# Weighing values in 64 by 32 tiles, and exchanging softmax statistics by ScalarE copies

## The chip, the cores and the metric

The kernel runs on one core of a Trainium2 chip. A core has a matrix engine (TensorE, "PE" in the profile, with its weight loads as "PEld"), VectorE (DVE), ScalarE (ACT) and GpSimd (POOL), each with its own queue of instructions that it works through in order, and SyncE (SP), which issues most DMAs here. The engines wait for each other by semaphores. The metric is the time of one execution in microseconds. Before the change it is 1120.16 us, the median of three runs (1119.69 to 1120.71).

## The reference

A transformer block over x of shape (2, 1024, 256), all in fp32, with 16 heads of 64 and a context of 154 rows of 192:

```python
h = _layernorm(x, ln1_g, ln1_b)
x = _attention(h, h, sa_wq, sa_wk, sa_wv, sa_wo, sa_bo) + x
h = _layernorm(x, ln2_g, ln2_b)
x = _attention(h, cond_emb, ca_wq, ca_wk, ca_wv, ca_wo, ca_bo) + x
h = _layernorm(x, ln3_g, ln3_b)
p = h @ ff_w1 + ff_b1
a, gate = (p[..., :D_FF], p[..., D_FF:])
h = a * jax.nn.gelu(gate, approximate=False) @ ff_w2 + ff_b2
return h + x
```

Attention is the usual one: scores q k^T / 8, softmax over the keys, and the weights times the values, for each head; then the output projection and its bias. The change lies in the self-attention, where queries and keys are both the 1024 rows.

## The kernel before

Heads are worked on in pairs: 2 batches times 8 pairs are 16 units. A unit is two halves of 512 queries, and a half is four slots (`SH`), so the self-attention has 16 x 8 = 128 slots (`SA`). One slot takes 128 queries, in two groups of 64 (`scores`, called twice). A group's score tile has 128 partitions, four quarters of 32. Quarter a4 holds 32 queries against one half of the keys: quarters 0 and 1 hold the same 32 queries against keys 0 to 511 and 512 to 1023, and quarters 2 and 3 do the same for the next 32 queries. So each query's softmax is spread over two neighbouring quarters, and their maxima and sums have to be brought together. The score matmuls use TensorE as 8 tiles of 64 rows by 32 columns (L483).

A slot goes through these steps:

- TensorE: scores of both groups into two PSUM tiles (`ps_s`, two buffers, so scores of the next slot wait for this slot's exponentials).
- VectorE: negated maxima of both groups into `st` (L645, in `self_first`).
- ScalarE: four exponentials with these maxima as bias; each also sums its output (L494, `exponents`, with a record of its own for reading the accumulator). Maxima and sums stand in `st[:, 0]`, eight numbers per partition.
- `exchange`: each quarter gets its neighbour's eight numbers in `st[:, 1]`, by four DMAs on SyncE's queue (L504).
- `join`, one slot later: GpSimd forms the differences of the maxima (`dd`, L512 to L514), ScalarE their exponentials (`ee`, L516), GpSimd the joint sums (`zz` L518, `den` L520).
- `reciprocals`, after that slot's transposes: VectorE's `rd` (L591), then GpSimd scales the four blocks of exponentials in place (L595).
- `turn_groups`, another slot later: VectorE transposes them in 32 by 32 blocks into `pT` (L609).
- `weigh`: when a half is done, its values are weighed in two parts (`self_values`, L530), in slots 2 and 3 of the next half. The operands' partitions pair query quarters with keys, so `v` is held twice, once with its partition halves swapped. Before the change the tiles are 64 by 64: for each key block four matmuls, two row halves by two heads.

Nothing reorders the work: the loop over p writes the order of each engine's queue by hand (`manual_schedule`). In slot p TensorE does the scores of p and then either weighing, or a piece of other work (projections of queries, keys and values of the next unit, L352 and L383; output projections, L457; layer-norm transposes, L270). VectorE's order is: maxima of p, transposes of p-2's exponentials, an addition of an output projection to `x` where there is one (L464), `rd` of p-1, layer-norm statistics where there are some (L230, L231, L246). ScalarE's order is: copies of the last piece of work out of PSUM (`stores`, such as L367, L375, L392, L630), exponentials of p, `ee` of p-1. `then` in `self_first` writes the order of `exponents`, `scale_groups` (which calls `join`) and `exchange`.

SyncE's queue also carries the loads of weights ahead of their use, and the swaps of `v`'s halves (L399, L400).

After the self-attention come the cross-attention (48 slots) and the feed-forward; neither is changed.

Of the kernel before, what the change touches and what calls it, by code (L numbers as in the profile page):

```python
# [18 lines left out]
def tile_transformer_block(ctx: ExitStack, tc: tile.TileContext, a: dict, out: bass.AP):  # L19
    nc = tc.nc  # L20
# [7 lines left out]
    DH = 64  # L28
# [11 lines left out]
    KB = 32  # L40
# [3 lines left out]
    QG = 2 * KB  # L44
    TP = NB * KB
    NM = P // QG
    QH = S // 2
    GH = QH // QG
    NK = HB // KB
# [45 lines left out]
    row_of, r = {}, 0  # L95
# [10 lines left out]
    for n in names[:2]:  # L106
        for r0 in range(0, P, HR):
            (nc.scalar if n == names[0] else nc.sync).dma_start(
                out=cols[r0:r0 + HR, row_of[n]:row_of[n] + NH],
                in_=w[n].rearrange("(r p) -> p r", p=HR),  # L110
# [365 lines left out]
    def scores(u, q, k, g):  # L476
        sc = ps_s.tile([P, 2, HB], F32, tag="s", name=f"s_{u}")
        for a4 in range(4):
            a2, h = divmod(a4, 2)
            for j in range(2):  # L480
                r = slice(j * DH, (j + 1) * DH)
                c = g * QG + a2 * KB
                nc.tensor.matmul(  # L483
                    sc[a4 * KB:(a4 + 1) * KB, j, :], lhsT=q[r, c:c + KB],
                    rhs=k[r, h * HB:(h + 1) * HB], start=True, stop=True,
                    tile_position=(j * DH, a4 * KB),
                )
        return sc

    def exponents(u, sc, st, i):  # L490

        pr = pp_.tile([P, 2, HB], F32, tag="P", name=f"p_{u}")
        for j in range(2):
            nc.scalar.activation(  # L494
                pr[:, j, :], sc[:, j, :], AF.Exp, bias=st[:, 0, 0, i, j:j + 1],
                accum_out=st[:, 0, 1, i, j:j + 1],
            )
        return pr

    def exchange(st):  # L500

        for a4 in range(4):
            o4 = a4 ^ 1
            nc.sync.dma_start(  # L504
                out=st[a4 * KB:(a4 + 1) * KB, 1], in_=st[o4 * KB:(o4 + 1) * KB, 0]
            )

    def join(u, st):

        dd = small.tile([P, 2, 4], F32, tag="dd", name=f"dd_{u}")  # L510
        neg = st[:, :, 0].rearrange("p s i j -> p s (i j)")
        nc.gpsimd.tensor_tensor(dd[:, 0, :], neg[:, 1, :], neg[:, 0, :], ALU.subtract)  # L512
        nc.gpsimd.tensor_tensor(dd[:, 1, :], neg[:, 0, :], neg[:, 1, :], ALU.subtract)
        nc.gpsimd.tensor_scalar(dd, dd, 0.0, 1.0, op0=ALU.min, op1=ALU.mult)  # L514
        ee = small.tile([P, 2, 4], F32, tag="ee", name=f"ee_{u}")
        nc.scalar.activation(ee, dd, AF.Exp)  # L516
        zz = small.tile([P, 2, 4], F32, tag="zz", name=f"zz_{u}")
        nc.gpsimd.tensor_tensor(zz, ee, st[:, :, 1].rearrange("p s i j -> p s (i j)"), ALU.mult)  # L518
        den = small.tile([P, 4], F32, tag="den", name=f"den_{u}")
        nc.gpsimd.tensor_tensor(den, zz[:, 0, :], zz[:, 1, :], ALU.add)  # L520
        return ee, den

    def weigh(po, v, pT, t):

        for e in range(2):
            for a2 in range(2):
                r = slice(a2 * QG, (a2 + 1) * QG)
                n = 2 * t + (e ^ a2)
                for j in range(2):
                    nc.tensor.matmul(  # L530
                        po[a2][j * DH:(j + 1) * DH, :QH // 2],
                        lhsT=v[r, t, e, j * DH:(j + 1) * DH], rhs=pT[r, j * NK + n, :],
                        start=(t == 0 and e == 0), stop=(t == NT - 1 and e == 1),
                        tile_position=(a2 * QG, j * DH),
                    )


# [47 lines left out]
    def scale_groups(u, st, members):  # L585

        ee, den = join(u, st)

        def reciprocals():
            rd = small.tile([P, 4], F32, tag="rd", name=f"rd_{u}")  # L590
            nc.vector.reciprocal(rd, den)  # L591
            for i, pr in enumerate(members):
                for j in range(2):
                    c = 2 * i + j
                    nc.gpsimd.tensor_scalar(  # L595
                        pr[:, j, :], pr[:, j, :], rd[:, c:c + 1], ee[:, 0, c:c + 1],
                        op0=ALU.mult, op1=ALU.mult,
                    )
                groups.append(pr)

        return reciprocals
# [11 lines left out]
    def self_values(h, part):  # L613

        b, pr = units[h // 2]
        if part == 0:
            bank = sum_tile if h < 2 * NU - 1 else mm_tile
            halves[h, "po"] = [bank(f"po_{h}_{a2}") for a2 in range(2)]
            if pr % HP == 0 and h % 2 == 0:
                oT["sa", b, pr // HP] = pt_.tile([P, HP, S], F32, tag="oT", name=f"o_sa{b}_{pr}")  # L620
        po = halves[h, "po"]
        for t in range(NT // 2 * part, NT // 2 * (part + 1)):
            weigh(po, qk["sa", b, pr][2], halves[h], t)
        if part == 0:
            return None
        dst = oT["sa", b, pr // HP][:, pr % HP, (h % 2) * QH:(h % 2 + 1) * QH]

        def store():
            for a2 in range(2):
                nc.scalar.copy(  # L630
                    dst.rearrange("p (g a i) -> p g a i", a=2, i=KB)[:, :, a2, :],
                    po[a2][:, :QH // 2].rearrange("p (g i) -> p g i", i=KB),
                )

        return store

    def self_first(p):

        b, pr = units[p // (2 * SH)]
        g = p % (2 * SH)  # L640
        q, k, _ = qk["sa", b, pr]
        st = small.tile([P, 2, 2, 2, 2], F32, tag="st8", name=f"st_{p}")
        sc = [scores(f"{p}_{i}", q, k, 2 * g + i) for i in range(2)]
        for i in range(2):
            nc.vector.tensor_reduce(st[:, 0, 0, i, :], sc[i], AX.X, ALU.max, negate=True)  # L645

        def then():
            members = [exponents(f"{p}_{i}", sc[i], st, i) for i in range(2)]
            late = scale_groups(*joins.pop(0)) if joins else None
            exchange(st)  # L650
            joins.append((p, st, members))
            return late

        return then
# [323 lines left out]
    with tc.manual_schedule():  # L978
# [57 lines left out]
        for p in range(SA):  # L1036
# [21 lines left out]
            if h == 0 or hg < LAG:  # L1058
# [4 lines left out]
                ui, n = divmod(p, 2 * SH)  # L1063
# [8 lines left out]
        for c in range(CA):  # L1072
# [13 lines left out]
            ui, n = divmod(c, len(CG))  # L1086
# [52 lines left out]
            elif n == 2:  # L1139
# [3 lines left out]
                elif ui == HP:  # L1143
                    wo["ca"] = const.tile([P, NPAIR, D], F32, tag="wo", name="ca_wo")
                    later[:0] = [lambda i=i: nc.sync.dma_start(
                        out=wo["ca"][:, i, :], in_=w["ca_wo"][i * P:(i + 1) * P, :])
# [65 lines left out]
```

## Time and profile before

| | |
|---|---|
| median of three runs | 1120.16 us |
| the profiled execution, its own time | 1119.22 us |
| its span, first to last instruction | 1117.4 us |
| TensorE busy | 1103.5 us (99%) |
| VectorE busy | 855.7 us (77%) |
| GpSimd busy | 681.0 us (61%) |
| ScalarE busy | 629.5 us (56%) |
| scores L483, 4096 records | 251.6 us |
| weighing L530, 4096 records | 235.8 us |
| exponentials L494, 512 | 344.8 us |
| scalings L595, 512 | 385.6 us |
| transposes L609, 256 | 302.2 us |
| maxima L645, 256 | 301.1 us |
| `st<-st` DMAs, 512 | 1.0 KB each, 1.8 us to landing |
| granted TensorE clock | 1.000 |

Busy time of a group is the union of its instructions' time, and "mean" is that of one instruction. Matmuls overlap in the array: a matmul record of 64x512 has a mean of 594 ns, yet 32 of them start and pass in under 2 us. So for TensorE the distance from one start to the next says more than durations. An fp32 matmul of the program shows as two records, each with a weight load. The first maxima of the self-attention start at 18.8 us, the last at 715.8 us. In the stretch from 20 to 717 us TensorE is busy for 692.5 us, VectorE for 630.5, GpSimd for 520.7 and ScalarE for 460.7. In the timeline, instructions of one kind that follow each other are merged into a line with their count.

### The profile page before, as it was taken

Reading aid. Unit: us, or ns where it says so; the run is one execution under the profiler, and the core shown is the slowest. Engines: PE = TensorE matmul, PEld = TensorE weight load, DVE = VectorE, ACT = ScalarE, POOL = GpSimd, SP = SyncE. Lnnn points to the kernel's source line nnn. Section 1 sums busy time; section 2 is a strip of 40 time slices with the busy share of each in tenths; the row PEclk is TensorE's granted clock in tenths of the full one; section 3 lists DMA queues with packets and bytes.
Section 4 is the critical chain, followed back from the end, with each engine's and each line's share of the span. In section 5 each row is a group of like instructions: output and inputs, shape, how many; then the busy total and the mean of one; then the engine's idle time right before and its main releaser. Section 6 shows DMA issues by size and latency. Waiting matters only on the chain.

```text
span 1117.4 us, 36668 instructions
## 1 busy us (share of the span) xinstructions
PE 1103.5 (99%) x14340; PEld 686.5 (61%) x14340; DVE 855.7 (77%) x1205; ACT 629.5 (56%) x2030; POOL 681.0 (61%) x1584
## 2 busy tenths in 40 slices
PE   8999999999999999999999999999999999999998
PEld 5445545545545455455455455476776777888887
DVE  4889999898998899999989989868777875412212
ACT  4666666766666666667666765665555553121111
POOL 2777777777777777777777777766656653220000
PEclk9999999999999999999999999999999999999999
DMA  3222212111111012011111111146665453000000
GB/s 85 70 57 50 55 27 51 48 34 41 32 31 42 22 41 46 13 42 39 24 41 32 31 32 26 25 95 158 160 157 125 114 115 79 10 11 10 20 10 19
DMA packets 102318, 59.14 MB, mean 53 GB/s; under 512 B 31994, under 2 KB 92930, under 8 KB 102146
## 3 DMA queue, kind: packets, MB, share of 16 engines
q1 hardware_dynamic: 100914, 56.15, 21.3%
q8 instruction: 113, 1.85, 0.7%
q10 hardware_dynamic: 1232, 0.66, 0.2%
q14 instruction: 59, 0.48, 0.1%
HBM read 27.12 MB, written 2.10 MB: 26 GB/s over the span
## 4 chain that ended last, share of the span: by engine, by line
PE 92%; ACT 2%; DVE 2%; DMA 1%; POOL 1%; SPq 1%; issue 1%; DVEq 0%; ACTq 0%; POOLq 0%
PE s L483 20%; PE po L530 20%; PE pa L933 10%; PE py_sa L457 5%; PE pv_sa L383 5%; PE py_ca L457 5%; PE pf L956 5%; PE pk_sa L352 4%; PE pq_sa L352 4%; PE pq_ca L352 4%; PE poc L851 4%; PE sc L772 3%; ACT p L494 2%; PE ph_ln L270 1%; PE pv_ca L733 1%; DVE st L645 1%
## 5 line engine op out<-in xcount | busy, mean ns | idle before, releaser
L494 ACT ACTIVATE p<-s,st 128x512 f32<-128x512 f32 x512 | 344.8, 686 | 199.0 <-DVE st L645 190.6
L595 POOL TENSOR_SCALAR p<-p,rd,ee 128x512 f32<-128x512 f32 x512 | 385.6, 768 | 47.6 <-DVE rd L591 46.3
L645 DVE TENSOR_REDUCE st<-s 128x2 f32<-128x1024 f32 x256 | 301.1, 1217 | 26.9 <-PE s L483 13.5
L609 DVE STREAM_TRANSPOSE pT<-p 128x1024 f32<-128x1024 f32 x256 | 302.2, 1218 | 0.3 <-POOL p L595 0.3
L483 PE MATMUL s<-k_sa,q_sa 64*32 64x512 f32 x4096 | 251.6, 594 | 5.0 <-ACT p L494 4.3
L530 PE MATMUL po<-pT,v_sa 64*64 64x256 f32 x4096 | 235.8, 380 | 0.9 <-DVE pT L609 0.9
L530 PEld LDWEIGHTS po<-pT,v_sa 64*64 64x64 f32 x4096 | 150.6, 133 | 109.3 <-issue 31.2
L483 PEld LDWEIGHTS s<-k_sa,q_sa 64*32 64x32 f32 x4096 | 66.8, 106 | 126.3 <-issue 68.2
L799 POOL TENSOR_SCALAR p<-p,rden 128x154 f32<-128x154 f32 x256 | 96.8, 399 | 76.0 <-DVE rden L796 75.6
L788 ACT ACTIVATE p<-sc,neg 128x154 f32<-128x154 f32 x256 | 96.1, 405 | 83.3 <-DVE rden L796 78.1
L942 DVE SCALAR_TENSOR_TENSOR u<-pa,cols,gate 128x256 f32<-128x256 f32 x64 | 31.0, 484 | 123.1 <-ACT gate L939 123.1
L933 PE MATMUL pa<-hT_ln,wf 128*128 128x256 f32 x512 | 121.1, 380 | 0.2 <-ACT p L788 0.2
L939 ACT ACTIVATE gate<-pa,cols 128x256 f32<-128x256 f32 x64 | 30.3, 474 | 147.8 <-PE pa L933 146.0
L933 PEld LDWEIGHTS pa<-hT_ln,wf 128*128 128x128 f32 x512 | 96.9, 190 | 13.9 <-issue 0.8
L494 ACT ACTIVATION_READ_ACCUMULATOR p<-s,st 128x1 f32 x512 | 103.8, 203 | 0.0
L383 PEld LDWEIGHTS pv_sa<-sa_wv,hT_ln 64*128 64x128 f32 x1024 | 58.8, 188 | 14.5 <-DMA st<-st 5.9
L518 POOL TENSOR_TENSOR zz<-ee,st 128x8 f32<-128x8 f32 x128 | 25.9, 202 | 65.6 <-ACT ee L516 65.6
L956 PE MATMUL pf<-wf,u 128*128 128x256 f32 x256 | 64.7, 379 | 0.0
L383 PE MATMUL pv_sa<-sa_wv,hT_ln 64*128 64x128 f32 x1024 | 62.0, 276 | 0.2 <-ACT v_sa L392 0.2
L457 PE MATMUL py_sa<-sa_wo,o_sa 128*128 128x256 f32 x256 | 59.7, 386 | 0.0
L457 PE MATMUL py_ca<-ca_wo,o_ca 128*128 128x256 f32 x256 | 59.7, 382 | 0.0
L457 PEld LDWEIGHTS py_sa<-sa_wo,o_sa 128*128 128x128 f32 x256 | 47.4, 190 | 17.8 <-issue 6.2
(87 smaller groups left out, 1250.6 us busy)
## 6 DMA issues: line engine op xcount, KB each, us to landing
wf<-pT_ca SPq DMA_DIRECT2D x128, 128.0 KB, 2.4
st<-st SPq DMA_DIRECT2D x512, 1.0 KB, 1.8
v_sa<-v_sa SPq DMA_DIRECT2D x32, 256.0 KB, 3.5
sa_wq<-in_L_xattn_sa_wq_dram SPq DMA_DIRECT2D x32, 128.0 KB, 2.8
sa_wk<-in_L_xattn_sa_wk_dram SPq DMA_DIRECT2D x32, 128.0 KB, 2.9
sa_wv<-in_L_xattn_sa_wv_dram SPq DMA_DIRECT2D x32, 128.0 KB, 2.9
ca_wq<-in_L_xattn_ca_wq_dram SPq DMA_DIRECT2D x32, 128.0 KB, 3.3
wf<-in_L_xattn_ff_w_dram SPq DMA_DIRECT2D x12, 256.0 KB, 4.2
```

Of the source, the lines that this page charges most:

```text
L352: nc.tensor.matmul(pq[r][f:f + m, at:at + n], lhsT=wt[own, c, f:f + m], rhs=h[own, c, t0:t0 + n], start=(c == 0), stop=(c == NH - 1), tile ...
L383: nc.tensor.matmul(pv[r][:, i * P:(i + 1) * P], lhsT=h[own, c, i * P:(i + 1) * P], rhs=wt[own, c, :], start=(c == 0), stop=(c == NH - 1), ...
L457: nc.tensor.matmul(py[:, e * D:(e + 1) * D], lhsT=o[:, i, (t + e) * P:(t + e + 1) * P], rhs=wo[kind][:, g * HP + i, :], start=(i == 0), st ...
L483: nc.tensor.matmul(sc[a4 * KB:(a4 + 1) * KB, j, :], lhsT=q[r, c:c + KB], rhs=k[r, h * HB:(h + 1) * HB], start=True, stop=True, tile_positi ...
L494: nc.scalar.activation(pr[:, j, :], sc[:, j, :], AF.Exp, bias=st[:, 0, 0, i, j:j + 1], accum_out=st[:, 0, 1, i, j:j + 1],)
L530: nc.tensor.matmul(po[a2][j * DH:(j + 1) * DH, :QH // 2], lhsT=v[r, t, e, j * DH:(j + 1) * DH], rhs=pT[r, j * NK + n, :], start=(t == 0 an ...
L595: nc.gpsimd.tensor_scalar(pr[:, j, :], pr[:, j, :], rd[:, c:c + 1], ee[:, 0, c:c + 1], op0=ALU.mult, op1=ALU.mult,)
L609: nc.vector.transpose(halves[h][:, :, c:c + KB], groups.pop(0).rearrange("p j (n k) -> p (j n) k", k=KB))
L645: nc.vector.tensor_reduce(st[:, 0, 0, i, :], sc[i], AX.X, ALU.max, negate=True)
L799: nc.gpsimd.tensor_scalar(pr_[:, j, i, :T], pr_[:, j, i, :T], rden[:, j, i:i + 1], 1.0, op0=ALU.mult, op1=ALU.mult,)
L933: nc.tensor.matmul(pa[:, half, :TF * P], lhsT=w1[:, c, half * DF + f * P:half * DF + (f + 1) * P], rhs=h[:, c, t0 * P:(t0 + TF) * P], star ...
L956: nc.tensor.matmul(sums[blk][i][:, :D], lhsT=sums[blk, "u"][:, f, i * P:(i + 1) * P], rhs=w2[:, f, :], start=(f == 0), stop=(f == NF - 1),)
```

## The change

Three edits. The exchange is done by ScalarE copies of 32 partitions by 8 elements, where it was done by DMAs. It is called between the exponentials and `scale_groups`, where it was called after both. And the weighing uses tiles of 64 rows by 32 columns, as the scores do: each 64 by 64 matmul becomes two of 64 by 32 with the same moving operand. Numbers of later lines fall by two: L512 to L520 become L510 to L518, L530 becomes L528, L591 becomes L589, L609 becomes L607; L645 becomes L643.

```diff
@@ exchange
         for a4 in range(4):
             o4 = a4 ^ 1
-            nc.sync.dma_start(
-                out=st[a4 * KB:(a4 + 1) * KB, 1], in_=st[o4 * KB:(o4 + 1) * KB, 0]
-            )
+            nc.scalar.copy(st[a4 * KB:(a4 + 1) * KB, 1], st[o4 * KB:(o4 + 1) * KB, 0])
@@ weigh
                 n = 2 * t + (e ^ a2)
-                for j in range(2):
+                for d in range(0, 2 * DH, KB):
                     nc.tensor.matmul(
-                        po[a2][j * DH:(j + 1) * DH, :QH // 2],
-                        lhsT=v[r, t, e, j * DH:(j + 1) * DH], rhs=pT[r, j * NK + n, :],
+                        po[a2][d:d + KB, :QH // 2],
+                        lhsT=v[r, t, e, d:d + KB], rhs=pT[r, d // DH * NK + n, :],
                         start=(t == 0 and e == 0), stop=(t == NT - 1 and e == 1),
-                        tile_position=(a2 * QG, j * DH),
+                        tile_position=(a2 * QG, d),
                     )
@@ self_first, then
             members = [exponents(f"{p}_{i}", sc[i], st, i) for i in range(2)]
+            exchange(st)
             late = scale_groups(*joins.pop(0)) if joins else None
-            exchange(st)
             joins.append((p, st, members))
             return late
```

## The prediction

> **What bounds the kernel now.** I read the chain that ended last first, then the timeline of the self-attention stretch, engine by engine. The page's chain gives its shares by engine and by line:
>
> ```profile
> PE 92%; ACT 2%; DVE 2%; DMA 1%; POOL 1%; SPq 1%; issue 1%; DVEq 0%; ACTq 0%; POOLq 0%
> ```
>
> TensorE is the bound, with 8% left for anything else. The timeline (start in us, length in us, engine, line, instruction, count, and in brackets the idle time before) shows what TensorE does in two slots of one half:
>
> ```profile
> 319.10 1.95 PE L483 MATMUL s<-k_sa,q_sa 64*32 64x512 f32 x32
> 320.97 3.69 PE L530 MATMUL po<-pT,v_sa 64*64 64x256 f32 x64
> 324.59 1.95 PE L483 MATMUL s<-k_sa,q_sa 64*32 64x512 f32 x32
> 326.33 3.64 PE L352 MATMUL pq_sa<-hT_ln,sa_wq 64*32 64x512 f32 x64
> 329.76 1.92 PE L483 MATMUL s<-k_sa,q_sa 64*32 64x512 f32 x32
> 331.48 1.07 PE L352 MATMUL pk_sa<-hT_ln,sa_wk 64*32 64x512 f32 x16
> ```
>
> From start to start: scores ahead of weighing take 1.87 us, weighing 3.62, scores between two projections of their own tile shape 1.72 (329.76 to 331.48), and a projection of 64 records 3.43. Each fp32 matmul leaves two records. The array work of the projection (64 x 512 columns over 8 tiles) equals that of the weighing (64 x 256 over 4).
>
> What is not in the chain, but close behind it, is a loop through the other engines. Here is one slot in which nothing else holds it up:
>
> ```profile
> 287.29 2.36 DVE L645 TENSOR_REDUCE st<-s 128x2 f32<-128x1024 f32 x2
> ...
> 288.55 0.69 ACT L494 ACTIVATE p<-s,st 128x512 f32<-128x512 f32 x1 [1.18 <-DVE st L645]
> ...
> 289.57 2.36 DVE L609 STREAM_TRANSPOSE pT<-p 128x1024 f32<-128x1024 f32 x2
> ...
> 291.12 0.21 ACT L494 ACTIVATION_READ_ACCUMULATOR p<-s,st 128x1 f32 x1
> 291.22 0.22 ACT L516 ACTIVATE ee<-dd 128x8 f32<-128x8 f32 x1
> 291.32 1.08 ACT L375 COPY k_sa<-pk_sa 128x512 f32<-128x512 f32 x2
> ...
> 291.52 0.20 POOL L518 TENSOR_TENSOR zz<-ee,st 128x8 f32<-128x8 f32 x1 [0.57 <-ACT ee L516]
> 291.80 0.20 POOL L520 TENSOR_TENSOR den<-zz 128x4 f32<-128x4 f32 x1
> 292.03 0.18 DVE L591 RECIPROCAL rd<-den 128x4 f32<-128x4 f32 x1
> ...
> 292.33 2.36 DVE L645 TENSOR_REDUCE st<-s 128x2 f32<-128x1024 f32 x2
> ```
>
> The maxima of a slot (L645) release its exponentials; behind them on ScalarE stands `ee` of the slot before; `ee` releases `zz`, `den` and then the reciprocal `rd`; and `rd` stands in VectorE's queue ahead of the next slot's maxima. So the loop closes once per slot and takes 292.33 - 287.29 = 5.04 us. From the first maxima of slot 1 (22.8 us on the timeline) to those of slot 126 (709.7) there are 125 slots in 686.9 us, 5.50 each: the loop has 0.46 us to spare against TensorE.
>
> **The change, part by part.**
>
> *Weighing in 64 by 32 tiles.* Scores and weighing now have one tile shape, so the pair costs 1.72 + 3.43 in place of 1.87 + 3.62: 0.34 us less. Of 64 parts, 62 stand between scores (two are in the cross-attention, beside other shapes): 62 x 0.34 = 21 us, if TensorE remained the bound. The columns streamed stay the same; instructions double to 128 records a part, 27 ns each at 3.43 us. The bounds: at worst a record keeps today's spacing in this line, 3.62 / 64 = 57 ns, and a part takes 7.2 us; at best the part takes 3.43 us. I take the best, because in the scores, whose tile shape this is, the timeline merges 16 weight loads of 106 ns mean into 0.18 us, so starts are about 5 ns apart.
>
> *Exchange: 512 DMAs leave SyncE's queue.* A slot's four took 2.4 to 2.5 us of issue there. Nothing behind them becomes critical by going earlier. One wait goes:
>
> ```profile
> POOL dd L512 <- DMA st<-st: 45.8, 43, 13.7
> ```
>
> It delayed `ee` by about 1 us in a third of the slots. Those delays took the loop over 5.50 us in single slots; TensorE's lead covered nearly all of it, as its 92% says. I count its removal as nothing beyond what the new loop below contains.
>
> *Exchange: four ScalarE copies of 32 partitions by 8 elements per slot.* Their place decides. In the new order they stand on ScalarE between the last exponential and `ee`, inside the loop above. Queued behind them are `ee` and the stores of projections; waiting for `ee` are `zz`, `den`, `rd`, and, behind `rd` on VectorE, the next maxima. Step by step:
> - The first copy reads sums that the last accumulator read writes, and waits for its end: 291.12 + 0.21. A wait for one's own engine costs about 0.08 us (GpSimd: `zz` ends at 291.72, `den` starts at 291.80). So it starts at 291.41, where `ee` started at 291.22, overlapped: 0.19 us.
> - Each copy. The trace has no copy of 8 elements; the nearest in kind are copies to parts of the partitions:
>
> ```profile
> 751.38 0.76 ACT L742 COPY v_ca<-pv_ca 64x256 f32<-64x256 f32 x2
> 752.16 0.36 ACT L743 COPY v_ca<-pv_ca 32x256 f32<-32x256 f32 x1
> ```
>
> These two, then one, start 0.39 us apart, with a mean of 0.368: each begins only after the one before has ended. Copies over all 128 partitions do overlap:
>
> ```profile
> 281.26 0.63 ACT L630 COPY o_sa<-po 128x256 f32<-128x256 f32 x2
> ```
>
> At a mean of 0.372 these start 0.26 apart. A column costs (588 - 372) / 256 = 0.84 ns by the full-width rows, so 8 in place of 256 take 0.21 off: 0.18 us apart without overlap. With overlap it is 0.04 by the same subtraction, or 0.10 by the shortest gap seen in these lines (`ee` to the next copy, 291.22 to 291.32). Between 0.04 and 0.18 I take 0.18, from the rows that are nearest: they too move from one range of partitions to another. `ee`, full width again, follows the fourth after 0.10 to 0.18. Four: 0.69.
> - Sum: 0.19 + 0.69 = 0.88 us. The loop becomes 5.92.
>
> The Trainium skill ("ScalarE: Activation LUTs", section What ACT_TABLE_LOAD costs) gives 186 ns + 0.833 ns per element with immediate operands and says that ACTIVATEs back to back overlap by about 93 ns. By that, an estimate, copies of 8 elements start 0.10 us apart and the loop becomes 5.63; the L742 rows, which do not overlap, speak against applying it here.
>
> *What the loop carries besides.* `rd` used to be ready 0.1 us after the transposes; now VectorE idles about 1 us ahead of it, which hides the `x` additions (L464, 0.65) that stand there. The layer-norm statistics stand behind `rd` and lengthen the loop: 16 tiles in this stretch at 0.399 + 0.182, and 8 offsets at 0.246, about 11 us, some 10 with their overlaps. GpSimd (4 scalings in 3.0, then `dd` in 0.7) is done about 1 us before the late `ee`, so a bias addition of 0.73 still fits.
>
> *Sum.* 125 x 5.92 + 10 = 750 us against 686.9: +63. TensorE's new need, 686.9 - 21 = 666, is 5.33 per slot, below the loop; its saving turns into waiting. The profiled execution took 1119.2 us (span 1117.4), 0.9 under the median of 1120.16. 1119.2 + 63 = 1182; some start-up slots are longer for other reasons, so I say 1181.
>
> **The rivals.**
> - *The copies overlap with a floor of 0.10 us.* Loop 5.04 + 0.19 + 0.40 = 5.63; 125 x 5.63 + 10 = 714: +27, 1146 us. For: full-width copies and `ee` do so. Against: L742 and L743.
> - *The copies stream at 0.04 us, and the kernel ends faster.* Loop 5.04 + 0.19 + 0.16 = 5.39; 674 + 10 = 684: -3 and a bit, 1116 us. It decides from 5.41 us on, that is 0.05 us per copy. For: the slope of the full-width rows. Against: no gap that short in these lines, and the partial copies.
> - *TensorE cannot be fed 128 records a part.* The part decides above 5.92 - 1.72 = 4.2 us, 33 ns per record; at 57 ns a slot takes 1.72 + 7.2 = 8.9, and 62 slots at 3.0 over the loop add 186: about 1367 us. Against: the bursts of loads. For: nothing in this trace sustains 27 ns.
> - The Trainium skill ("TensorE: Matmul & The Clock Gate", section Wait — 56ns, not 53.3ns?) puts the floor between matmul starts at about 25 ns; as an estimate 128 of them are 3.2 us, just inside the 3.43. No row here shows that floor.
>
> **How the numbers follow.** The forecast (copies without overlap) 0.65; overlapping at 0.10 0.20; streaming and faster 0.08; TensorE short of instructions 0.05; the rest 0.02. The range takes in the first two with their bounds: low 1138 (rival one with most statistics hidden), high 1200 (0.15 us more in each slot: copies 0.20 apart, and a second wait of 0.08). A difference under 0.2% is about what a measurement of this kernel can't tell from no change; faster 0.07, same 0.03, slower 0.90.
>
> **What the profile after would show.** Right: maxima about 5.9 us apart in plain slots; `ee` about 0.8 us after the last accumulator read has ended; copies 0.18 us from start to start; VectorE idle about 1 us ahead of `rd`, released by `den`; waits of TensorE's scores for ScalarE; weighing near 3.43 us; no wait of `dd` for a DMA. Wrong: copies 0.1 us apart or less, TensorE still unbroken, or weighing far above 3.43.

## The result, and the profile after

The changed kernel takes 1175.38 us (median of four runs, 1175.11 to 1175.67) against 1119.93 for the kernel before (four runs): 1.0497 times as long, 95% interval 1.0479 to 1.0515. The forecast was 1181 us in a range of 1138 to 1200. The profiled execution took 1175.67 us, its span is 1173.9.

The page's chain that ended last, by engine and by line, has changed hands:

```profile
ACT 38%; PE 35%; DVE 14%; POOL 5%; issue 3%; DMA 0%; SPq 0%; DVEq 0%; ACTq 0%
ACT p L494 27%; DVE st L643 12%; PE pa L931 9%; ACT st L504 7%; PE py_ca L457 5%; PE pf L954 5%; PE pq_ca L352 4%; PE poc L849 3%; PE sc L770 3%; PE pk_sa L352 2%; ACT ee L514 2%; POOL zz L516 2%; POOL den L518 2%; PE s L483 1%; PE pv_ca L731 1%
```

TensorE went from 92% to 35%, which is about the share of the cross-attention and the feed-forward. In the self-attention the chain now runs through the exponentials, the maxima, the copies (L504), `ee`, `zz` and `den`: the loop of the prediction. One slot of it in the timeline:

```profile
316.11 2.36 DVE L643 TENSOR_REDUCE st<-s 128x2 f32<-128x1024 f32 x2
...
317.37 0.69 ACT L494 ACTIVATE p<-s,st 128x512 f32<-128x512 f32 x1 [1.00 <-DVE st L643]
...
318.38 2.36 DVE L607 STREAM_TRANSPOSE pT<-p 128x1024 f32<-128x1024 f32 x2
...
319.94 0.21 ACT L494 ACTIVATION_READ_ACCUMULATOR p<-s,st 128x1 f32 x1
320.19 0.81 ACT L504 COPY st<-st 32x8 f32<-32x8 f32 x4
...
321.03 0.21 ACT L514 ACTIVATE ee<-dd 128x8 f32<-128x8 f32 x1
...
321.32 0.20 POOL L516 TENSOR_TENSOR zz<-ee,st 128x8 f32<-128x8 f32 x1 [1.36 <-ACT ee L514]
321.60 0.20 POOL L518 TENSOR_TENSOR den<-zz 128x4 f32<-128x4 f32 x1
321.83 0.18 DVE L589 RECIPROCAL rd<-den 128x4 f32<-128x4 f32 x1 [1.08 <-POOL den L518]
321.94 2.36 DVE L643 TENSOR_REDUCE st<-s 128x2 f32<-128x1024 f32 x2
```

The period is 321.94 - 316.11 = 5.83 us, where it was 5.04 in an undisturbed slot. Up to the last accumulator read nothing has moved (3.83 us after the maxima, before and after). The copies start 0.04 us after that read has ended and take 0.81; `ee` starts 1.09 after the read's start, where it was 0.10, so it comes 0.99 later. And at the end `rd` to the next maxima takes 0.11 us, where it took 0.30: a gain that the prediction didn't have. From the first maxima of slot 1 (23.19 us) to those of slot 126 (765.05) the stretch takes 741.9 us, against 686.9: 55.0 us more, which is the whole difference between the medians (55.4).

TensorE waits now. From its timeline, and from the list of waits, after and then before (engine, line, for whom, us in total, times, longest):

```profile
321.09 3.67 PE L528 MATMUL po<-pT,v_sa 64*32 64x256 f32 x128
324.70 1.09 PE L483 MATMUL s<-k_sa,q_sa 64*32 64x512 f32 x16
326.04 1.09 PE L483 MATMUL s<-k_sa,q_sa 64*32 64x512 f32 x16 [0.24 <-ACT p L494]
```

```profile
POOL zz L516 <- ACT ee L514: 168.9, 128, 3.9
...
PEld s L483 <- ACT p L494: 151.2, 203, 2.2
...
DVE rd L589 <- POOL den L518: 127.3, 128, 3.6
```

```profile
POOL zz L518 <- ACT ee L516: 65.6, 128, 1.6
...
PEld s L483 <- ACT p L494: 39.2, 87, 2.5
DVE rd L591 <- POOL den L520: 36.2, 55, 3.4
```

The scores of the two groups, one block before, now start 1.34 us apart (324.70 and 326.04): each waits for the exponentials that hold its PSUM buffer. `rd` waits for `den` in every one of the 128 slots, about 1 us each, where it had waited in 55.

### The profile page after: what moved, and what is told of

The parts are those of the page before. It is cut to its first block, busy times and chain, and to the rows that moved or that the text cites. A ratio compares the mean times of both kernels' runs of the same rounds, so it can differ in the third digit from the quotient of the medians.

```text
span 1173.9 us, 43766 instructions
## 1 busy us (share of the span) xinstructions
PE 1129.0 (96%) x18436; PEld 713.3 (61%) x18436; DVE 849.3 (72%) x1205; ACT 734.5 (63%) x2542; POOL 679.2 (58%) x1584
## 4 chain that ended last, share of the span: by engine, by line
ACT 38%; PE 35%; DVE 14%; POOL 5%; issue 3%; DMA 0%; SPq 0%; DVEq 0%; ACTq 0%
ACT p L494 27%; DVE st L643 12%; PE pa L931 9%; ACT st L504 7%; PE py_ca L457 5%; PE pf L954 5%; PE pq_ca L352 4%; PE poc L849 3%; PE sc L770 3%; PE pk_sa L352 2%; ACT ee L514 2%; POOL zz L516 2%; POOL den L518 2%; PE s L483 1%; PE pv_ca L731 1%
## 5 line engine op out<-in xcount | busy, mean ns | idle before, releaser
L483 PE MATMUL s<-k_sa,q_sa 64*32 64x512 f32 x4096 | 283.5, 599 | 26.1 <-ACT p L494 23.7
L643 DVE TENSOR_REDUCE st<-s 128x2 f32<-128x1024 f32 x256 | 300.8, 1216 | 3.4 <-PE s L483 3.0
L607 DVE STREAM_TRANSPOSE pT<-p 128x1024 f32<-128x1024 f32 x256 | 302.3, 1218 | 0.2 <-POOL p L593 0.2
L528 PE MATMUL po<-pT,v_sa 64*32 64x256 f32 x8192 | 242.0, 376 | 0.9 <-DVE pT L607 0.9
L528 PEld LDWEIGHTS po<-pT,v_sa 64*32 64x32 f32 x8192 | 175.4, 106 | 75.2 <-issue 22.7
L483 PEld LDWEIGHTS s<-k_sa,q_sa 64*32 64x32 f32 x4096 | 62.9, 105 | 175.1 <-ACT p L494 151.2
L589 DVE RECIPROCAL rd<-den 128x4 f32<-128x4 f32 x128 | 22.8, 178 | 127.3 <-POOL den L518 127.3
L504 ACT COPY st<-st 32x8 f32<-32x8 f32 x512 | 99.7, 195 | 8.5
L352 PE MATMUL pk_sa<-hT_ln,sa_wk 64*32 64x512 f32 x960 | 61.8, 592 | 6.6 <-ACT q_sa L367 6.6
```

Source lines behind the costliest of these rows:

```text
L352: nc.tensor.matmul(pq[r][f:f + m, at:at + n], lhsT=wt[own, c, f:f + m], rhs=h[own, c, t0:t0 + n], start=(c == 0), stop=(c == NH - 1), tile ...
L483: nc.tensor.matmul(sc[a4 * KB:(a4 + 1) * KB, j, :], lhsT=q[r, c:c + KB], rhs=k[r, h * HB:(h + 1) * HB], start=True, stop=True, tile_positi ...
L504: nc.scalar.copy(st[a4 * KB:(a4 + 1) * KB, 1], st[o4 * KB:(o4 + 1) * KB, 0])
L528: nc.tensor.matmul(po[a2][d:d + KB, :QH // 2], lhsT=v[r, t, e, d:d + KB], rhs=pT[r, d // DH * NK + n, :], start=(t == 0 and e == 0), stop= ...
L607: nc.vector.transpose(halves[h][:, :, c:c + KB], groups.pop(0).rearrange("p j (n k) -> p (j n) k", k=KB))
```

## The experiments

**The tiles alone.** The exchange stays a DMA, in its old place.

```diff
-                for j in range(2):
+                for d in range(0, 2 * DH, KB):
...
-                        tile_position=(a2 * QG, j * DH),
+                        tile_position=(a2 * QG, d),
```

> Only the 64 by 32 tiles of the weighing; the exchange by DMAs and its place stay as before. My theory: the loop through VectorE, ScalarE and GpSimd stays at 5.04 us a slot, below TensorE's new need of 5.33, so most of the 0.34 us for each of 62 parts comes through: 1099 to 1110 us, weighing 3.43 us from start to start. Rival, that 128 records a part cost TensorE more than the shared tile shape saves: 1120 us or above, weighing above 3.6 us.

1115.8 us, ratio 0.9961 (0.9947 to 0.9975): faster, but by 5 us, below what my theory gave. TensorE's part came out as expected, by its timeline:

```profile
322.32 3.66 PE L530 MATMUL po<-pT,v_sa 64*32 64x256 f32 x128
325.77 1.92 PE L483 MATMUL s<-k_sa,q_sa 64*32 64x512 f32 x32
327.49 3.81 PE L352 MATMUL pq_sa<-hT_ln,sa_wq 64*32 64x512 f32 x64
```

Weighing takes 3.45 us from start to start (3.62 before), the scores 1.72. So 128 records pass at 27 ns each, and the rival that they can't is out. What took the rest has no run of its own. The list of waits and the chain name candidates:

```profile
POOL dd L512 <- DMA st<-st: 45.3, 42, 14.2
```

```profile
PE 67%; ACT 8%; DMA 7%; DVE 5%; POOL 5%; SPq 4%; issue 3%; DVEq 0%; POOLq 0%; ACTq 0%
```

The late DMAs of the exchange hold up `dd`, and with it `ee`, in a third of the slots, as they did before. Then TensorE's 5.50 us a slot covered most of that; with less to do it covers less. DMA and its queue now have 11% of the chain in place of 2%, and ScalarE, VectorE and GpSimd together 18% in place of 5%. The prediction had treated those waits as nothing. The loop here also holds the 0.19 us that a later experiment finds. How the loss divides between the two was not measured.

**The copies alone.** Weighing in 64 by 64 tiles.

```diff
-            nc.sync.dma_start(
-                out=st[a4 * KB:(a4 + 1) * KB, 1], in_=st[o4 * KB:(o4 + 1) * KB, 0]
-            )
+            nc.scalar.copy(st[a4 * KB:(a4 + 1) * KB, 1], st[o4 * KB:(o4 + 1) * KB, 0])
...
+            exchange(st)
             late = scale_groups(*joins.pop(0)) if joins else None
-            exchange(st)
```

> Only the exchange by ScalarE copies ahead of the joint exponentials ee; the weighing in 64 by 64 tiles as before. My theory: the loop rules with 5.83 us a slot whatever TensorE saves, so the time is that of the changed kernel: 1172 to 1179 us, copies 0.2 us apart, ee about 0.87 us after the last accumulator read. Rival, that the tiles have a share in the loss: below 1168 us.

1175.44 us, ratio 1.0490 (1.0475 to 1.0506): the changed kernel's time within 0.1 us. The stretch from slot 1 to slot 126 takes 741.8 us against 741.9. The whole loss is the exchange's, and the tiles' gain is fully hidden beneath it.

**The copies behind `ee`.** All of the change, but with the call in its old place.

```diff
             members = [exponents(f"{p}_{i}", sc[i], st, i) for i in range(2)]
-            exchange(st)
             late = scale_groups(*joins.pop(0)) if joins else None
+            exchange(st)
```

> The changed kernel with the copies behind ee in ScalarE's queue, where the DMAs were called before. My theory: it was the place in the loop that cost, not the copies' time; the loop returns to 5.04 less the 0.19 us that the maxima no longer wait for DMA semaphores, 4.85 us, TensorE is the bound again with 5.33 a slot: 1096 to 1106 us. Rival, that 0.8 us more work on ScalarE per slot delays the next exponentials wherever it stands: 1140 us or above.

1107.51 us, ratio 0.9881 (0.9866 to 0.9896). One line's move is worth 68 us: the same copies, as long as before (99.7 us of ScalarE's time in both), cost nothing like that once `ee` doesn't stand behind them. The rival is out. It stays 1.5 us above my range. In the slots with weighing TensorE takes 5.17 us from one part to the next, as it should, but in others it waits for ScalarE's copies out of PSUM, which now stand behind the exchange:

```profile
327.67 3.72 PE L352 MATMUL pk_sa<-hT_ln,sa_wk 64*32 64x512 f32 x57 [0.18 <-ACT q_sa L367]
...
332.85 0.38 PE L528 MATMUL po<-pT,v_sa 64*32 64x256 f32 x1
...
338.02 0.38 PE L528 MATMUL po<-pT,v_sa 64*32 64x256 f32 x1
```

```profile
PEld pk_sa L352 <- ACT q_sa L367: 18.9, 30, 1.4
```

**The same with 64 by 64 tiles.** The edit is the DMA-to-copy one alone, in its old place.

```diff
-            nc.sync.dma_start(
-                out=st[a4 * KB:(a4 + 1) * KB, 1], in_=st[o4 * KB:(o4 + 1) * KB, 0]
-            )
+            nc.scalar.copy(st[a4 * KB:(a4 + 1) * KB, 1], st[o4 * KB:(o4 + 1) * KB, 0])
```

> Copies behind ee as in the run with both, but the weighing in 64 by 64 tiles as before. My theory: TensorE is the bound with 5.50 us a slot, plus the banks that come free later; the late DMAs of before are gone: 1118 to 1130 us, so the tiles are worth 11 to 22 us where the loop is short. Rival, that the gain of the run with both came from the exchange: below 1112 us.

1123.49 us, ratio 1.0022 (1.0013 to 1.0032). So the copies behind `ee` gain nothing by themselves, and the tiles are worth 16.0 us on top of them (1123.49 to 1107.51), 5 us with the DMAs, and nothing with the copies ahead of `ee`. The same edit has three values, by what stands next to it.

**Ahead of the next slot's exponentials.** The copies go where ScalarE waits for the maxima anyway, behind the copies out of PSUM.

```diff
+            if joins:
+                exchange(joins[0][1])
             members = [exponents(f"{p}_{i}", sc[i], st, i) for i in range(2)]
-            exchange(st)
             late = scale_groups(*joins.pop(0)) if joins else None
...
             if c == 0:
+                exchange(joins[0][1])
                 drain.append(scale_groups(*joins.pop(0)))
```

> The changed kernel with a slot's copies ahead of the next slot's exponentials and behind the copies out of PSUM, where ScalarE waits for the maxima anyway. My theory: behind ee the copies delayed the copies out of PSUM, and TensorE waited for their banks about 0.4 us in slots 1 and 4 of each unit; here they delay neither ee nor those: 1096 to 1104 us. Rival, that in slots with long copies out of PSUM they push the exponentials back by as much: 1106 us or above.

1100.43 us, ratio 0.9811 (0.9797 to 0.9826): the fastest of all, 21 us below the kernel before and 75 below the changed one. ScalarE's timeline shows the place:

```profile
321.44 0.21 ACT L514 ACTIVATE ee<-dd 128x8 f32<-128x8 f32 x1
321.54 1.09 ACT L367 ACTIVATE q_sa<-pq_sa 128x512 f32<-128x512 f32 x2
322.65 0.81 ACT L504 COPY st<-st 32x8 f32<-32x8 f32 x4
323.62 0.69 ACT L494 ACTIVATE p<-s,st 128x512 f32<-128x512 f32 x1 [0.15 <-DVE st L643]
```

After the four copies ScalarE still waits 0.15 us for the maxima: they cost nothing in this slot. ScalarE waits for the maxima in 103 of the 128 slots here, in 120 before, so in some slots the room is used up. The stretch takes 667.1 us, where the prediction put TensorE's new need at 666, and TensorE is back at the head of the chain:

```profile
PE 86%; ACT 7%; DVE 3%; POOL 2%; issue 1%; DMA 1%; DVEq 0%; ACTq 0%
```

**Four copies over all partitions.** Why are the copies 0.2 us apart? In the first try each of the four was made 128 partitions wide, in place:

```diff
-            nc.scalar.copy(st[a4 * KB:(a4 + 1) * KB, 1], st[o4 * KB:(o4 + 1) * KB, 0])
+            nc.scalar.copy(st[:, 1], st[:, 0])
```

> The changed kernel with each of the four copies over all 128 partitions, in the same place; nothing is exchanged between the quarters (each gets its own statistics), so the softmax sums are left unjoined. My theory: copies over parts of the partitions can't overlap, full-width ones do: 0.10 us apart in place of 0.20, the loop 0.42 us shorter, 1120 to 1130 us. Rival, that a copy of 8 elements takes 0.2 us from start to start whatever its partitions: 1173 to 1178 us.

1168.72 us, ratio 1.0429 (1.0413 to 1.0444), between the two forecasts. It doesn't tell: the four write the same place, and each waited on a semaphore for the one before, 0.23 us from start to start.

```profile
323.01 0.89 ACT L504 COPY st<-st 128x8 f32<-128x8 f32 x4
323.81 0.20 ACT L514 ACTIVATE ee<-dd 128x8 f32<-128x8 f32 x1
```

So the question was put again with three of them going to a tile that nothing reads:

```diff
+        spread = small.tile([P, 3, 2, 2, 2], F32, tag="spread", name="spread")
+        nc.scalar.copy(st[:, 1], st[:, 0])
+        for i in range(3):
+            nc.scalar.copy(spread[:, i], st[:, 0])
-        for a4 in range(4):
-            o4 = a4 ^ 1
-            nc.scalar.copy(st[a4 * KB:(a4 + 1) * KB, 1], st[o4 * KB:(o4 + 1) * KB, 0])
```

> The changed kernel with four copies over all 128 partitions: one of each quarter's own statistics to where the neighbour's belong, three to a tile that nothing reads, so that none waits for another (with four to one place each waited for the one before). Nothing is exchanged, the sums are left unjoined. My theory: copies over parts of the partitions don't overlap, full-width ones do: 0.05 to 0.10 us apart, the loop 0.4 to 0.6 us shorter, 1110 to 1126 us. Rival, that a copy of 8 elements takes 0.2 us from start to start whatever its partitions: 1170 to 1178 us.

1121.63 us, ratio 1.0003 (0.9993 to 1.0012).

```profile
318.27 0.69 ACT L494 ACTIVATE p<-s,st 128x512 f32<-128x512 f32 x1 [1.96 <-DVE st L644]
...
321.09 0.20 ACT L503 COPY st<-st 128x8 f32<-128x8 f32 x1
321.19 0.39 ACT L505 COPY spread<-st 128x8 f32<-128x8 f32 x3
321.49 0.20 ACT L515 ACTIVATE ee<-dd 128x8 f32<-128x8 f32 x1
323.65 0.69 ACT L494 ACTIVATE p<-s,st 128x512 f32<-128x512 f32 x1 [1.96 <-DVE st L644]
```

Now they start 0.10 us apart, each of 0.19 us, so they do overlap, and `ee` follows 0.40 after the first start (0.84 in the changed kernel). The loop becomes 5.38 us (323.65 - 318.27). So 0.44 of the 0.99 us by which `ee` came later was the missing overlap.

**Width, or change of partitions?** Two kernels, run once each, have the three spare copies over a quarter each: always partitions 0 to 31 in one, each time the next quarter in the other.

```diff
-            nc.scalar.copy(spread[:, i], st[:, 0])
+            nc.scalar.copy(spread[:KB, i], st[:KB, 0])
```

> As the run with four full-width copies that don't wait for each other, but three of them over partitions 0 to 31 alone, always the same. Nothing is exchanged, the sums are left unjoined. Theory one, that a copy over fewer partitions than the engine has never overlaps: the three 0.21 us from start to start, the loop near 5.7 us. Theory two, that it is the change of partitions from one copy to the next: the three 0.10 us apart among themselves, the loop near 5.5 us or below.

```diff
-            nc.scalar.copy(spread[:, i], st[:, 0])
+            r = slice(i * KB, (i + 1) * KB)
+            nc.scalar.copy(spread[r, i], st[r, 0])
```

> The same, with the three copies over partitions 0 to 31, 32 to 63 and 64 to 95, each from and to its own quarter. Nothing is exchanged, the sums are left unjoined. Both theories: 0.21 us from start to start. If it is below 0.15 us, then neither holds, and what kept the copies of the change apart is that they read one quarter and write another.

1122.12 us for the first and 1162.0 for the second, in one run each, beside 1122.67 for the kernel before. The first's timeline and then the second's:

```profile
321.44 0.20 ACT L503 COPY st<-st 128x8 f32<-128x8 f32 x1
321.55 0.39 ACT L505 COPY spread<-st 32x8 f32<-32x8 f32 x3
321.85 0.20 ACT L515 ACTIVATE ee<-dd 128x8 f32<-128x8 f32 x1
```

```profile
320.42 0.20 ACT L503 COPY st<-st 128x8 f32<-128x8 f32 x1
320.52 0.61 ACT L506 COPY spread<-st 32x8 f32<-32x8 f32 x3
321.15 0.21 ACT L516 ACTIVATE ee<-dd 128x8 f32<-128x8 f32 x1
```

Three copies of one quarter take 0.39 us together, as three of full width do, and the full-width `ee` behind them overlaps too; three that move from quarter to quarter take 0.61, and `ee`, back at partition 0, starts only after the last has ended. So neither the width nor the crossing from one quarter to another keeps copies apart; a change of the first partition does. One rival is left: in every pair that stayed apart, one of the two starts at a partition other than 0, and no run has two in a row that start at the same partition other than 0. What the engine does at such a change stays open too.

**The DMAs as well.** Where do the 0.19 us between `rd` and the next maxima come from? The four DMAs were added to the changed kernel, from the same statistics to a tile that nothing reads.

```diff
+        spare_st = small.tile([P, 2, 2, 2], F32, tag="spare_st", name="spare_st")
         for a4 in range(4):
             o4 = a4 ^ 1
             nc.scalar.copy(st[a4 * KB:(a4 + 1) * KB, 1], st[o4 * KB:(o4 + 1) * KB, 0])
+            nc.sync.dma_start(
+                out=spare_st[a4 * KB:(a4 + 1) * KB], in_=st[o4 * KB:(o4 + 1) * KB, 0]
+            )
```

> The changed kernel, and the four DMAs of before as well, from the same statistics to a tile that nothing reads. My theory: the maxima then wait again for four DMA semaphores ahead of their first one, 0.19 us a slot in the loop: 0.30 us from the start of the reciprocal to the next maxima in place of 0.11, 1195 to 1200 us. Rival, that the shorter gap came from elsewhere: 1174 to 1178 us.

1198.35 us, ratio 1.0685 (1.0669 to 1.0701): 23.0 us above the changed kernel, 0.18 a slot.

```profile
318.12 0.18 DVE L593 RECIPROCAL rd<-den 128x4 f32<-128x4 f32 x1 [1.09 <-POOL den L522]
318.42 2.36 DVE L647 TENSOR_REDUCE st<-s 128x2 f32<-128x1024 f32 x2
```

The 0.30 are back. The maxima overwrite a tile that DMAs have read four slots ago, and must wait for them; the DMAs are as a rule long done, yet the waits themselves take time. The views of the maxima's line show them, before, then after, then in this run (durations are least, median and most, in ns):

```profile
L645 DVEq EVENT_SEMAPHORE  x372: 21/50/921, 39.8 to 714.6; - x186
```

```profile
L643 DVEq EVENT_SEMAPHORE  x124: 21/50/50, 41.9 to 770.8; - x124
```

```profile
L647 DVEq EVENT_SEMAPHORE  x372: 21/50/50, 41.7 to 793.6; - x186
```

Three extra wait instructions a slot became one, and are three again here, though none of them lasts over 50 ns. Two more of them make 0.19 us, so each takes about 0.10 us of the loop.

## Why the prediction was right

**The bound.** Right. The loop through VectorE, ScalarE and GpSimd took over from TensorE in the self-attention, by the path that the prediction named, and the chain shows it. The run with the copies alone gives the same time as both edits, and the move of the call by one line gives 68 us back.

**The size of the loop.** 5.92 forecast, 5.83 measured. That they are so close is in part luck: two errors cancel in part. The step "0.19 + 0.69 = 0.88" was too small: the wait for the engine's own end took 0.04 in place of 0.08, but each copy 0.205 in place of 0.18, and `ee` came 0.22 after the start of the fourth, where the prediction took 0.10 to 0.18; together `ee` moved by 0.99. The other error is a term that was missing: the maxima no longer wait for DMA semaphores, 0.19 us in the loop. The prediction had looked for what stands behind the DMAs in their queue and for who waits for their data (`dd`), and not at who waits to overwrite what they read. 5.04 + 0.99 - 0.19 is 5.84.

**The choice between 0.04, 0.10 and 0.18 per copy.** The nearest rows (L742 and L743) were the right guide, and for the right reason: they too move from one range of partitions to another. The Trainium skill's overlap of about 93 ns for ACTIVATEs back to back ("ScalarE: Activation LUTs", section What ACT_TABLE_LOAD costs) holds in the two runs whose copies start at one partition (0.10 us apart, 0.19 long) and not where the first partition changes (0.205 apart). Had the copies been of that kind, the time would have been the 1122 us of those runs, not the rival's 1146: its loop of 5.63 us is 0.25 above the 5.38 measured there, nearly all of it the wait (0.04) and the missing DMA semaphores (0.19).

**TensorE's saving.** 0.34 us a part forecast; 1.72 and 3.45 us from start to start make it 0.32. It was rightly expected to turn into waiting. Where the loop is short it comes through: the fastest run's stretch of 667.1 us against a forecast need of 666.

**What was counted as nothing.** For the changed kernel this held: no wait for the DMAs is left and the loop rules. For the tiles alone three quarters of the gain stayed away, and by the chain the late DMAs are among the reasons. The prediction's "about 1 us in a third of the slots" reads its line too high: one of the 43 waits is 13.7 us long, and the other 42 have 0.76 us each.

**The rest of the stretch.** 741.9 - 125 x 5.825 leaves 13.8 us where the forecast had 10 for the layer-norm statistics; the first two slots took 1.4 of it, and I haven't followed the rest. The forecast's 63 us became 55: the shorter loop took off 12, and this rest put 4 back.

## What to carry to other kernels

A short instruction is priced by what stands behind it in its queue: 0.8 us of copies per slot cost 55 us ahead of the one instruction that closes a loop through three engines, and next to nothing in a gap of the same queue. Before moving work between engines, follow the queue order around to the place where it returns to its own start, and compare that period with the bound engine's. When a transfer goes away, look also at who waits to overwrite what it reads.

## What the runs showed of the hardware

- On ScalarE, consecutive instructions that start at one partition overlap: copies of 8 elements, 0.19 us long, start 0.10 us apart, whether 32 or 128 partitions wide. Where the first partition changes (0, 32, 64 and back), the next starts only after the end of the one before: 0.205 us apart. Before the run I had put this down to the width. Two in a row at one partition other than 0 were not tried.
- Waits cost time even when what they wait for is long done: four DMA semaphores ahead of one VectorE instruction meant two more wait instructions and took 0.19 us a slot in a loop (23 us in all).
- TensorE took 128 records a part, each with its weight load, at 27 ns per record (3.45 us); a switch between 64 by 32 and 64 by 64 tiles had cost 0.15 to 0.17 us each. That it is the switch and not the larger tile fits the scores, whose own shape never changed: 1.72 us from their start to weighing in 64 by 32 tiles, 1.87 to weighing in 64 by 64.
